# Two attention layers on one core: the second layer's row sums brought to 32 rows per tile by four transfers, one 128x4 product per block, and output products in pairs

## The chip, the cores and the metric

The kernel runs on one core of a Trainium2 chip. The metric is device time in microseconds (us) of one execution; less is better. Before the change the median of three runs is 3128.35 us (3128.15 to 3134.23).

## What is computed

Four images of 4096 tokens with 256 channels pass through two attention layers, all in fp32:

```python
q, k, v = x @ Wq + bq, x @ Wk + bk, x @ Wv + bv            # layer 0; q, k: 32 wide, v: 256
x = gamma * softmax(q @ k.T) @ v + x
g, f, v = x @ Wg + bg, x @ Wf + bf, x @ Wh + bh            # layer 1; g, f: 32 wide, v: 128
x = x + (softmax(g @ f.T) @ v) @ Wo + bo
```

No maximum is taken off before the exponential. The softmax's denominator is divided out at the end, so the kernel needs, for each query, the sum of the exponentials over 4096 keys.

## The kernel before

The program is one long unrolled list of 1024 **steps**: four images `b`, in each layer 0 and then layer 1. Layer 0 has 16 blocks `j` of 256 queries with 8 steps each, layer 1 has 8 blocks of 512 queries with 16 steps `i` each; a step of layer 1 takes 256 keys against 512 queries. In a step the TensorE (PE) makes the scores `st` (L621), the ScalarE (ACT) their exponential `p` (L638), and the PE multiplies by the values (L713 in layer 1, L689 in layer 0). Half of the steps of layer 1, the split ones, work with a coarse `high` from ACT (L631) and two remainders `low` (L659) and `d` (L664) from the VectorE (DVE). A split step gives the PE four short passes at once, and two more with the next step; the others give it four long ones.

**Sums.** The `p` of a block are added over its steps. Some steps are added into `p_sum` by the DVE (L678). Those named in `MOVED_SUMS`, or in `MOVED_IMAGE` and `MOVED_LAST` for the last image, are added into `p_sum_moved` by accumulating DMAs on the queue of GpSimd (POOL, L650, L652; L654 joins two such sums in the last image). After the block, `add_moved` (L778) and `fold` (L782) bring all into `sums`: 128 rows by 512 queries, where the 128 rows are still to be added. `later_sums` is a planner's list of these DVE additions, each with a cost and a latest step; `tensor_clock` and `vector_clock` say when one may go.

**Outputs.** A block's outputs are made in the next block. `output(t)` has three stages for each of four 128-query tiles: `multiply` puts the product of `o` and `wo` (L799, 128x256) and the product of the tile of `sums` with a column of ones (L800, 128x1, which adds the 128 rows) into one PSUM buffer `pso`; `divide` is the reciprocal on the DVE (L803); `give` is the scaled copy to `y` on ACT (L807), and an accumulating DMA from POOL that adds `y` to the rows of `out` (L809). This is done for 31 blocks. The last block of all has code of its own (`last_sums`, `last_denominators`, `last_outputs`: L838 to L872), which is not changed.

**Order.** From step 8 on the order is written by hand: each engine, and each DMA queue (SP's and POOL's), takes its instructions in program order. `put(n, slot, ...)` hangs a stage on step n: slot "a" is at the step's start, slot "b" behind the scores of the step two ahead and ahead of the step's own products. `OUT_AT = (9, 10, 12, 13)` are the steps of the next block in which the four tiles are multiplied; `divide` follows in slot "a" and `give` in slot "b" of the next step. The last block of an image has its outputs in steps 1 to 4 of the next image's layer 0, the block before the last of all in `LAST_OUT_AT`. PSUM buffers of the tag `side` (two) are shared by `pso` and the projections `psv` (L497) and `psqk` (L446); SBUF buffers of the tag `small` (four) by `y`, `x_res` and others. SP's queue carries the loads for the projections (`xT_again` L917, `squares` L290, `x_res` L1007), POOL's the accumulating DMAs and the loads of `q` and `k` (L543).

Of the kernel before, what the change touches and what calls it, by code (L numbers as in the profile page):

```python
# [50 lines left out]
F32 = mybir.dt.float32  # L51
F32R = mybir.dt.float32r
I32 = mybir.dt.int32
AF = mybir.ActivationFunctionType
ALU = mybir.AluOpType
AX = mybir.AxisListType

P = 128
QB = 512
QB0 = 256  # L60
NT = QB // P
S = 32
# [1 line left out]
EPS = 2.0**-12  # L64
UP = 2.0**12
AHEAD = 3
OUT_AT = (9, 10, 12, 13)
LAST_OUT_AT = (5, 6, 7, 8)
MOVED_AT = 1
KEEP, AHEAD_OF = 3, 1.0  # L70
Q_AHEAD = 6
# [179 lines left out]
def fast_path(ctx: ExitStack, tc: tile.TileContext, x, w0, w1, wo, bo, gamma, out, off):  # L251

    nc = tc.nc
    B, N, C = x.shape
# [9 lines left out]
    NS = QB0 // P  # L264
# [7 lines left out]
    const = ctx.enter_context(tc.tile_pool(name="const", bufs=1))  # L272
    data = ctx.enter_context(tc.tile_pool(name="data", bufs=1))
    work = ctx.enter_context(tc.tile_pool(name="work", bufs=2))
    dram = ctx.enter_context(tc.tile_pool(name="dram", bufs=1, space=bass.MemoryType.DRAM))
# [25 lines left out]
    rows = {}  # L301
# [18 lines left out]
    nc.sync.dma_start(ident_dram, ident)  # L320
    ones = const.tile([P, 1], F32, name="ones")
    nc.vector.memset(ones, 1.0)

    inverse = const.tile([P, 2, B * N // P], F32, name="inverse")
    seen_v = const.tile([P, 2, B * NH], F32, name="seen_v")
# [8 lines left out]
    wo_sb = const.tile([P, C], F32, name="wo")  # L334
# [20 lines left out]
    def side_psum(name):  # L355
        return ps_side.tile([P, QB], F32, tag="side", name=name)
# [3 lines left out]
    for j in range(NB):  # L360
        forms = {}
        for what, col in (("h", 1.0), ("l", 0.0), ("d", -EPS)):
            t = const.tile([P, NT, W], F32R, tag=f"v0{what}_{j}", name=f"v0{what}_{j}")
# [24 lines left out]
    q_t, moved_sums, first_p, later_sums, v_whole = {}, {}, [], [], {}  # L388
# [3 lines left out]
    def put(n, slot, *stages):  # L392
        todo.setdefault((n, slot), []).extend(stages)
# [167 lines left out]
    last_block = B * PER_IMAGE - NI[1]  # L561
# [30 lines left out]
    def small(name):  # L592
        return work.tile([P, C], F32, tag="small", bufs=4, name=name)
# [171 lines left out]
    def take_first_two(b, j, acc):  # L765

        o = []
        for h in range(QB // QB0):
            o.append(work.tile([P, W], F32, tag="o", name=f"o_{b}_{j}_{h}"))
            nc.scalar.activation(o[h][:, :QB0], acc[0][:, h * QB0 : (h + 1) * QB0], AF.Copy, scale=1.0 + EPS)  # L770
        return o

    def end_second(b, j, acc, p_sum, o, n_next):
        key = f"{b}_{j}"
        sums = [None]

        def add_moved():
            nc.vector.tensor_add(p_sum, p_sum, moved_sums[b, j, 0])  # L778

        def fold():  # L780
            sums[0] = work.tile([P, QB], F32, tag="sums", bufs=1, name=f"sums_{key}")
            nc.vector.tensor_add(sums[0].rearrange("p (a n) -> p a n", n=QB0), p_sum[:, :NS, :], p_sum[:, NS:, :])  # L782

        wait = j < NQ[1] - 1
        if not wait:
            while later_sums:
                later_sums.pop(0)[2]()
        for h in range(QB // QB0):
            nc.vector.tensor_add(o[h][:, :QB0], o[h][:, :QB0], acc[1][:, h * QB0 : (h + 1) * QB0])  # L789

        def output(t):
            tok = slice(t * P, (t + 1) * P)
            n = (b * N + j * QB) // P + t
            held = {}

            def multiply():
                held["ps"] = ps = side_psum(f"pso_{key}_{t}")
                part = o[t // NS][:, t % NS * P : (t % NS + 1) * P]
                nc.tensor.matmul(ps[:, :C], part, wo_sb, start=True, stop=True)  # L799
                nc.tensor.matmul(ps[:, C : C + 1], sums[0][:, tok], ones[:, :1], start=True, stop=True)  # L800

            def divide():
                nc.vector.reciprocal(inverse[:, 1, n : n + 1], held["ps"][:, C : C + 1])  # L803

            def give():
                y = small(f"y_{key}_{t}")
                nc.scalar.activation(y, held["ps"][:, :C], AF.Copy, scale=inverse[:, 1, n : n + 1])  # L807
                row = j * QB + t * P
                nc.gpsimd.dma_start(out[b, row : row + P, :], y, accum_op=ALU.add)  # L809

            return multiply, divide, give

        out_at = (1, 2, 3, 4) if not wait else OUT_AT if n_next < last_block else LAST_OUT_AT
        if wait:
            put(n_next + MOVED_AT, "b", lambda: later_sums.append((1.15, n_next + MOVED_AT + 3, add_moved, None)))
            put(n_next + MOVED_AT, "b", lambda: later_sums.append((0.6, n_next + MOVED_AT + 4, fold, f"p_sum_{b}_{j}")))
        else:
            put(n_next, "b", add_moved, fold)
        for t in range(NT):
            multiply, divide, give = output(t)  # L820
            at = n_next + out_at[t]
            put(at, "b", multiply)
            put(at + 1, "a", divide)
            put(at + 1, "b", give)

    ending = {}

# [64 lines left out]
    def put_all(n, at, stages):  # L892
        for where, stage in zip(at.split(), stages):
            put(n + int(where[:-1]), where[-1], stage)
# [63 lines left out]
    acc, p_sum, o = None, None, []  # L958
    tensor_clock, vector_clock = 0.0, 0.0
# [27 lines left out]
    for n, s in enumerate(steps):  # L987
        now[0] = n
        b, l, j = s.b, s.l, s.j
# [4 lines left out]
        if s.first:  # L994
            o = []
# [6 lines left out]
        if l == 0 and s.i == NI[0] - 3:  # L1002
            x_res[b, j] = []
            for t in range(NS):
                x_res[b, j].append(small(f"x_res_{b}_{j}_{t}"))
                row = (j * NS + t) * P
# [7 lines left out]
        if ahead is not None and ahead.first:  # L1014
            k = (ahead.b, ahead.l, ahead.j * (QB0, QB)[ahead.l] // QB)
# [13 lines left out]
        if l == 0:  # L1029
            s.cut_both()  # L1030
            after.cut_low()
        else:
            cost = 1.9 if s.split else 2.2
            tensor_clock += cost + 1.7 * (b + 1 < B and s.i in (3, 7)) + 0.63 * (j > 0 and s.i in OUT_AT)
            vector_clock = max(vector_clock, tensor_clock - cost)
            s.cut_both()
            after.cut_low()
            vector_clock += 1.15 * (s.split + after.split)
            if n < len(steps) - 2:
                s.add_up(p_sum)  # L1040
        if l == 1:
# [4 lines left out]
            if s.last:  # L1046
                o = take_first_two(b, j, acc)
# [5 lines left out]
            while later_sums and (later_sums[0][1] <= n or vector_clock + later_sums[0][0] <= tensor_clock + AHEAD_OF):  # L1053
                took, _, issue, _ = later_sums.pop(0)
# [12 lines left out]
            if n == len(steps) - 1:  # L1067
                last_outputs(acc, o)
            elif s.last:
                vector_clock += 0.8  # L1070
                end_second(b, j, acc, p_sum, o, n + 1)
# [23 lines left out]
def tile_two_attention_layers(tc: tile.TileContext, *args):  # L1095
    nc = tc.nc
    with tc.tile_pool(name="flag", bufs=1) as pool:
        off = pool.tile([1, 1], I32, name="off")
        fast_path(tc, *args, off)
        flag = nc.values_load(off[0:1, 0:1], min_val=0, max_val=4 * P, skip_runtime_bounds_check_because="a count")  # L1100
        with tc.If(flag < 1, preferred_fallthrough_block=False, label="in_range") as usual:
            pass
        with usual.Else():
            general_path(tc, *args)
# [40 lines left out]
```

## Time and profile before

| | us |
|---|---|
| median of three runs | 3128.35 |
| the profiled execution, its own time | 3129.13 |
| its span in the trace | 3127.4 |
| a block of layer 1, images 0 to 2 (640.0 to 678.5) | 38.5, of it PE 38.50, DVE 34.27, ACT 27.99, POOL 10.50 |
| a block of layer 1, image 3 (2973.5 to 3008.5) | 35.0, of it PE 35.00, DVE 29.64, ACT 25.64, POOL 12.92 |
| layer 0 of image 1 (836.2 to 1332.3) | 496.1, of it PE 494.50, DVE 444.44, ACT 349.77 |

The granted TensorE clock is 0.999 over the span. Blocks are counted here from the copy of the first accumulator (L770) that ends a block's products. Times in the profile are from the span's start. PE instructions in fp32 with full precision are recorded as two passes (L799 and L800: 124 products, 248 records); DMA groups give the KB of one transfer and the median us from issue to landing.

### The profile page before, as it was taken

The numbers are of one execution on the slowest core, as the hardware profiler recorded it, in microseconds if no ns is written. First come the engines' busy times: TensorE is split into PE (matmuls) and PEld (weight loads), VectorE is DVE, ScalarE is ACT, GpSimd is POOL, SyncE is SP. The second block draws the span as 40 slices with busy tenths as digits, with TensorE's granted clock in tenths as the row PEclk, the third lists the DMA queues.
The fourth block names the chain that finished last, engine by engine and source line by source line (L and its number), as shares of the span: only waits on it lengthen the run. The fifth ranks groups of instructions, "written<-read, shape, count | busy, mean of one in ns | idle before, by whom it ended". The sixth has DMA issues, their size and how long they took to land.

```text
span 3127.4 us, 55023 instructions
## 1 busy us (share of the span) xinstructions
PE 3093.8 (99%) x20052; PEld 2692.9 (86%) x20052; DVE 2732.4 (87%) x3328; ACT 2203.5 (70%) x2900; POOL 791.8 (25%) x1157
## 2 busy tenths in 40 slices
PE   8999999999999999999999999999999999999998
PEld 7999999666799999866679999986668999997665
DVE  6899889988888989998889988998888888888887
ACT  7767777777677777777767777677776666667775
POOL 4111113222411111422241111132234111123332
PEclk9999999999999999999999999999999999999999
DMA  4344455656644444656554444465565333337776
GB/s 124 75 89 89 84 96 115 127 115 118 125 85 84 93 89 87 128 121 118 117 110 92 84 89 90 88 133 115 115 128 97 63 70 72 60 76 158 154 154 140
DMA packets 441606, 325.86 MB, mean 104 GB/s; under 512 B 264466, under 2 KB 386196, under 8 KB 441332
## 3 DMA queue, kind: packets, MB, share of 16 engines
q0 software_dynamic: 112272, 196.49, 34.9%
q1 hardware_dynamic: 328148, 125.47, 16.8%
q8 instruction: 162, 2.65, 0.4%
q14 instruction: 112, 0.92, 0.1%
q10 hardware_dynamic: 912, 0.33, 0.1%
HBM read 128.45 MB, written 95.49 MB: 72 GB/s over the span
## 4 chain that ended last, share of the span: by engine, by line
PE 88%; DVE 3%; DMA 3%; issue 2%; ACT 2%; POOL 1%; SPq 0%; DVEq 0%; POOLq 0%; ACTq 0%
PE acc L689 23%; PE acc_pair L689 23%; PE acc L713 21%; PE st L621 14%; PE psv L497 4%; DMA p_sum_moved<-p 2%; PE psqk L446 2%; PE pso L799 1%; POOL k L543 1%; ACT p L638 0%; PE pso L800 0%; DVE d L664 0%; DVE low L659 0%; DVE p_sum L678 0%; ACT v0l L524 0%
## 5 line engine op out<-in xcount | busy, mean ns | idle before, releaser
L631 ACT ACTIVATE high<-st,down 128x1024 fp32r<-128x1024 f32 x651 | 728.2, 1119 | 686.9 <-PE st L621 609.1
L638 ACT ACTIVATE p<-st 128x1024 f32<-128x1024 f32 x1024 | 1028.9, 1021 | 20.3 <-DMA p_sum_moved<-p 9.3
L659 DVE TENSOR_TENSOR low<-p,high 128x1024 fp32r<-128x1024 f32 x565 | 690.7, 1223 | 144.4 <-ACT p L638 136.8
L664 DVE SCALAR_TENSOR_TENSOR d<-low,high 128x1024 fp32r<-128x1024 f32 x547 | 667.5, 1220 | 15.3 <-PE acc L713 0.7
L621 PE MATMUL st<-q,k 128*128 128x256 f32 (+1 forms) x3072 | 661.5, 323 | 0.6 <-DMA q<-qk_dram 0.5
L621 PEld LDWEIGHTS st<-q,k 128*128 128x128 f32 x3072 | 472.1, 189 | 57.5 <-issue 8.1
L713 PE MATMUL acc<-p,v 128*128 128x512 f32 (+1 forms) x1028 | 487.6, 596 | 0.8 <-DVE o L789 0.7
L689 PE MATMUL acc<-v0d,d 128*128 128x258 f32 x2048 | 336.5, 286 | 5.0 <-DVE d L664 4.7
L689 PE MATMUL acc<-v0h,high 128*128 128x258 f32 x2048 | 330.9, 284 | 1.2 <-ACT high L631 1.2
L689 PE MATMUL acc_pair<-v0l,low 128*128 128x256 f32 (+1 forms) x2048 | 329.9, 283 | 0.0
L689 PE MATMUL acc_pair<-v0h,high 128*128 128x258 f32 x2048 | 329.6, 283 | 0.0
L689 PE MATMUL acc<-v0l,low 128*128 128x256 f32 (+1 forms) x2048 | 328.1, 282 | 1.1 <-DVE low L659 0.8
L689 PE MATMUL acc_pair<-v0d,d 128*128 128x258 f32 x2048 | 328.8, 282 | 0.0
L754 POOL DMA_DIRECT2D out<-x x128 | 114.8, 897 | 839.3 <-DVE x L748 831.4
L713 PEld LDWEIGHTS acc<-p,v 128*128 128x128 f32 x1028 | 187.6, 189 | 143.1 <-issue 124.4
L678 DVE TENSOR_TENSOR p_sum<-p_sum,p 128x1024 f32<-128x1024 f32 x239 | 291.2, 1219 | 0.5
L689 PEld LDWEIGHTS acc<-v0d,d 128*128 128x128 f32 x2048 | 280.9, 189 | 7.8 <-DVE d L664 5.9
L689 PEld LDWEIGHTS acc<-v0h,high 128*128 128x128 f32 x2048 | 281.5, 189 | 3.0 <-ACT high L631 1.4
L689 PEld LDWEIGHTS acc<-v0l,low 128*128 128x128 f32 x2048 | 280.9, 189 | 2.6 <-DVE low L659 2.6
L689 PEld LDWEIGHTS acc_pair<-v0l,low 128*128 128x128 f32 x2048 | 282.4, 189 | 0.1
L689 PEld LDWEIGHTS acc_pair<-v0h,high 128*128 128x128 f32 x2048 | 281.9, 189 | 0.2 <-DVE o L733 0.2
L689 PEld LDWEIGHTS acc_pair<-v0d,d 128*128 128x128 f32 x2048 | 281.6, 189 | 0.0
(173 smaller groups left out, 4231.6 us busy)
## 6 DMA issues: line engine op xcount, KB each, us to landing
p_sum_moved<-p POOLq DMA_DIRECT2D x207, 512.0 KB, 5.0
x_res<-in_x SPq DMA_DIRECT2D x128, 128.0 KB, 3.2
qk_dram<-qk_parts SPq DMA_DIRECT2D x128, 128.0 KB, 2.2
x_res<-bias POOLq DMA_DIRECT2D x128, 128.0 KB, 4.1
out<-bias SPq DMA_DIRECT2D x128, 128.0 KB, 4.0
out<-x POOLq DMA_DIRECT2D x128, 128.0 KB, 3.1
q<-qk_dram POOLq DMA_DIRECT2D x252, 64.0 KB, 4.0
out<-y POOLq DMA_DIRECT2D x124, 128.0 KB, 3.5
```

The lines of the kernel that those rows point to most:

```text
L446: nc.tensor.matmul(t["ps"], wqk[l][:, c, :], x_parts[key][n][:, c, :], start=(c == n == 0), stop=(c == NCC - 1 and n == 1),)
L497: nc.tensor.matmul(ps[:, n, :], xT[key][:, c, n * P : (n + 1) * P], wv[l][:, c, :], start=(c == 0), stop=(c == NCC - 1),)
L543: nc.gpsimd.dma_start(dst[n * D : (n + 1) * D, :], parts[h, which])
L621: nc.tensor.matmul(st[:, g, :], k_t[b, l, kt // NT][:, kt % NT * P : (kt % NT + 1) * P], q_t[b, l, j * n // QB][:, q0 : q0 + n], start=Tru ...
L631: nc.scalar.activation(self.high, s_flat, AF.Exp, bias=down)
L638: nc.scalar.activation(self.p, s_flat, AF.Exp)
L659: nc.vector.tensor_sub(self.low, self.p, self.high.bitcast(F32))
L664: nc.vector.scalar_tensor_tensor(self.d, self.low.bitcast(F32), -UP, self.high.bitcast(F32), ALU.mult, ALU.add)
L678: nc.vector.tensor_add(p_sum, other, self.p)
L689: nc.tensor.matmul(acc[2 * s + which][:, :width], p[:, g, s * P : (s + 1) * P], v0[self.i][v][:, g, :width], start=self.first and what != ...
L713: nc.tensor.matmul(acc[which].rearrange("p (a n) -> p a n", n=QB0)[:, cols, :], v_part[:, g, :], p[:, g * NS : (g + 1) * NS, :][:, cols, : ...
L754: nc.gpsimd.dma_start(out_rows(b, j, s), x_new, accum_op=ALU.add)
```

## The change

The 128 rows of `sums` are no longer added by the PE alone. `fold_rows` adds rows 64 to 127 onto rows 0 to 63 by an accumulating DMA on POOL's queue; `store_rows` writes the 64 rows to DRAM from SP's queue; `gather(0)` reads 32 of them back from SP's queue, so that tile t of the queries lies on partitions 32t to 32t+31 of a 128x128 buffer `rows`; `gather(1)` adds the other 32 by an accumulating DMA on POOL's queue. Each waits for the one before. Then one product of `rows` with a constant 128x4 matrix (`quarters`) gives the block's four columns of sums (`count`), and one reciprocal of 128x4 takes the place of four of 128x1. The output products of two tiles share one `pso` buffer. The stages have new steps: transfers in slots 5a, 5b, 6b, 7b, `count` in 11b, the pairs in 12b and 14b, each given one step later; behind an image's last block 1a, 1b, 2b, 3a, then 5b, 5b and 6b. The planner's two deadlines come one step earlier, and its cost for the outputs is 0.86 in two steps for 0.63 in four.

```diff
-OUT_AT = (9, 10, 12, 13)
-LAST_OUT_AT = (5, 6, 7, 8)
+OUT_AT = (11, 12, 14)
+FIRST_OUT_AT = (5, 5, 6)
+GATHER_AT = "5a 5b 6b 7b"
+FIRST_GATHER_AT = "1a 1b 2b 3a"
...
+    quarters = const.tile([P, NT], F32, name="quarters")
+    nc.vector.memset(quarters, 0.0)
+    for t in range(NT):
+        nc.vector.memset(quarters[t * S : (t + 1) * S, t : t + 1], 1.0)
...
+        def fold_rows():
+            nc.gpsimd.dma_start(sums[0][: P // 2, :], sums[0][P // 2 :, :], accum_op=ALU.add)
+
+        def store_rows():
+            held["dram"] = dram.tile([P // 2, QB], F32, name=f"sums_dram_{key}")
+            nc.sync.dma_start(held["dram"], sums[0][: P // 2, :])
+
+        def gather(k):
+            def issue():
+                if k == 0:
+                    held["rows"] = small(f"rows_{key}")[:, :P]
+                part = held["dram"][k * S : (k + 1) * S, :].rearrange("r (t q) -> t r q", q=P)
+                if k == 0:
+                    nc.sync.dma_start(held["rows"], part)
+                else:
+                    nc.gpsimd.dma_start(held["rows"], part, accum_op=ALU.add)
...
+        def count():
+            held["ps"] = ps = side_psum(f"ps_sums_{key}")
+            nc.tensor.matmul(ps[:, :NT], held["rows"], quarters, start=True, stop=True)
+
+        def divide():
+            nc.vector.reciprocal(inverse[:, 1, n : n + NT], held["ps"][:, :NT])
+
+        def output(h):
             def multiply():
-                held["ps"] = ps = side_psum(f"pso_{key}_{t}")
-                part = o[t // NS][:, t % NS * P : (t % NS + 1) * P]
-                nc.tensor.matmul(ps[:, :C], part, wo_sb, start=True, stop=True)
-                nc.tensor.matmul(ps[:, C : C + 1], sums[0][:, tok], ones[:, :1], start=True, stop=True)
+                held[h] = ps = side_psum(f"pso_{key}_{h}").rearrange("p (s c) -> p s c", c=C)
+                for s in range(NS):
+                    nc.tensor.matmul(ps[:, s, :], o[h][:, s * P : (s + 1) * P], wo_sb, start=True, stop=True)
             def give():
+                for s in range(NS):
...
-            put(n_next + MOVED_AT, "b", lambda: later_sums.append((1.15, n_next + MOVED_AT + 3, add_moved, None)))
-            put(n_next + MOVED_AT, "b", lambda: later_sums.append((0.6, n_next + MOVED_AT + 4, fold, f"p_sum_{b}_{j}")))
+            put(n_next + MOVED_AT, "b", lambda: later_sums.append((1.15, n_next + 3, add_moved, None)))
+            put(n_next + MOVED_AT, "b", lambda: later_sums.append((0.6, n_next + 4, fold, f"p_sum_{b}_{j}")))
...
+        put_all(n_next, gather_at, (fold_rows, store_rows, gather(0), gather(1)))
+        put(n_next + out_at[0], "b", count)
+        put(n_next + out_at[0] + 1, "a", divide)
+        for h, at in enumerate(out_at[1:]):
+            multiply, give = output(h)
+            put(n_next + at, "b", multiply)
+            put(n_next + at + 1, "b", give)
...
-            tensor_clock += cost + 1.7 * (b + 1 < B and s.i in (3, 7)) + 0.63 * (j > 0 and s.i in OUT_AT)
+            tensor_clock += cost + 1.7 * (b + 1 < B and s.i in (3, 7)) + 0.86 * (j > 0 and s.i in OUT_AT[1:])
```

More of the change, by code (lines that the diff above doesn't have):

```diff
@@ L789, in end_second @@
             nc.vector.tensor_add(o[h][:, :QB0], o[h][:, :QB0], acc[1][:, h * QB0 : (h + 1) * QB0])
[L791 to L794, printed above, removed]
-            def multiply():
-                held["ps"] = ps = side_psum(f"pso_{key}_{t}")
-                part = o[t // NS][:, t % NS * P : (t % NS + 1) * P]
[L799 to L803, printed above, removed]
-            def give():
[L806 to L811, printed above, removed]
@@ L813, in end_second @@
-        out_at = (1, 2, 3, 4) if not wait else OUT_AT if n_next < last_block else LAST_OUT_AT
+        held = {}
+        def fold_rows():
[12 more added lines that the diff above has]
+                    nc.gpsimd.dma_start(held["rows"], part, accum_op=ALU.add)
+            return issue
@@ new lines, in end_second @@
+        n = (b * N + j * QB) // P
+        def count():
[4 more added lines that the diff above has]
+        def output(h):
+            def multiply():
+                held[h] = ps = side_psum(f"pso_{key}_{h}").rearrange("p (s c) -> p s c", c=C)
+                for s in range(NS):
+                    nc.tensor.matmul(ps[:, s, :], o[h][:, s * P : (s + 1) * P], wo_sb, start=True, stop=True)
+            def give():
+                for s in range(NS):
+                    t = h * NS + s
+                    y = small(f"y_{key}_{t}")
+                    nc.scalar.activation(y, held[h][:, s, :], AF.Copy, scale=inverse[:, 1, n + t : n + t + 1])
+                    row = j * QB + t * P
+                    nc.gpsimd.dma_start(out[b, row : row + P, :], y, accum_op=ALU.add)
+            return multiply, give
@@ L814, in end_second @@
+        out_at, gather_at = (OUT_AT, GATHER_AT) if wait else (FIRST_OUT_AT, FIRST_GATHER_AT)
         if wait:
-            put(n_next + MOVED_AT, "b", lambda: later_sums.append((1.15, n_next + MOVED_AT + 3, add_moved, None)))
-            put(n_next + MOVED_AT, "b", lambda: later_sums.append((0.6, n_next + MOVED_AT + 4, fold, f"p_sum_{b}_{j}")))
+            put(n_next + MOVED_AT, "b", lambda: later_sums.append((1.15, n_next + 3, add_moved, None)))
+            put(n_next + MOVED_AT, "b", lambda: later_sums.append((0.6, n_next + 4, fold, f"p_sum_{b}_{j}")))
@@ L817, in end_second @@
         else:
             put(n_next, "b", add_moved, fold)
[L819 to L824, printed above, removed]
+        put_all(n_next, gather_at, (fold_rows, store_rows, gather(0), gather(1)))
[5 more added lines that the diff above has]
+            put(n_next + at + 1, "b", give)
```

## The prediction

> **What bounds the kernel now.** I read the shares of busy time first, then the busy time by stretches, then the chain of waits inside one block, then the DMA groups and the last block.
>
> ```profile
> PE 3093.8 (99%) x20052; PEld 2692.9 (86%) x20052; DVE 2732.4 (87%) x3328; ACT 2203.5 (70%) x2900; POOL 791.8 (25%) x1157
> ```
>
> A share over the whole span could hide a stage with another limit, so next come the stretches of one block of layer 1 in images 0 to 2, and of one in image 3 (columns: length, then busy PE, PEld, DVE, ACT, POOL, clock, DMA share, GB/s):
>
> ```profile
> 640.00:678.50 38.50, 38.50 (x145) 26.52 (x144) 34.27 (x38) 27.99 (x38) 10.50 (x14) 1.00 0.57 112
> ...
> 2973.50:3008.50 35.00, 35.00 (x129) 23.44 (x128) 29.64 (x32) 25.64 (x32) 12.92 (x17) 1.00 0.79 158
> ```
>
> The PE is never idle in either; the DVE has 4.2 us to spare in the first and 5.4 us in the second. Anything that leaves the PE here shortens the block, until something else is late. The chain inside such a block (start, us, what) tells what an output tile costs:
>
> ```profile
> 657.07 1.73 PE psv L497 x8
> ...
> 665.65 0.47 PE st L621 x2
> 666.12 0.43 PE pso L799 x2
> 666.55 0.12 PE pso L800 x2
> 666.67 1.05 PE acc L713 x4
> 667.71 0.46 PE st L621 x2
> ...
> 675.71 0.46 PE st L621 x2
> 676.17 0.93 PE acc L713 x4
> 677.10 0.47 PE st L621 x2
> ```
>
> From scores to scores a split step with an output takes 667.71 - 665.65 = 2.06 us, one without 677.10 - 675.71 = 1.39 us: an output tile costs 0.66 us (the long steps say the same: 3.30 against 2.65). The eight 256-column passes of `psv` take 1.73 us, 0.216 each, so the two passes of L799 are 0.43 us. What is left, **0.23 us, is the product with the ones**: 0.12 at its own place and 0.11 by which the product behind it comes later.
>
> **The change on the PE.** Per block three of four such products go; the fourth, now 128x4, I keep at 0.23 us (four columns, the same weight load). The wo products stay, four by 0.43; in pairs they stand as `psv`'s passes do, for 0.216 a pass. So 2.64 us become 1.95, a gain of 0.69 us; with the measured 0.224 (2.047 - 1.391 - 0.432, medians over all such steps) it is 0.67. For 30 blocks 20.2 us; the 31st is taken apart below. The nearest other price for a one-column product is the busy time of its group, 34.4 us for 124, 0.28 us each, which would make 25 us; its own 0.12 us alone would make 11 us. I take 20.2.
>
> The Trainium skill speaks against so much: "TensorE: Matmul & The Clock Gate", section "Back-to-back issue gap", gives a product of 1 to 64 columns some 25 ns, so 0.05 us in two passes; by that the whole gain would be 4.7 us, and the time about 3124. The rows above have 0.23 us, and decide.
>
> Three stalls of the PE go besides: in the last block of images 0 to 2 the outputs of steps 9 and 10 wait for a `side` buffer that `psv` of step 9 holds ("PE pso L799 <- DVE v0d L533: 2.7, 3"). The new steps are clear of it. But ACT there waits for `p_sum_moved` (1.4 us before 820.6), and that lateness may show at the next product, so I count 1.7 of 2.7 us.
>
> **DVE and ACT.** The DVE's order is unchanged but for three reciprocals fewer (0.48 us a block): the planner had issued `add_moved` and `fold` before both deadlines. So `sums` is ready when it was: the DVE ends L782 at 650.22 in the block of 640.0, at 2984.47 in that of 2973.5. In step 15 ACT now has two copies (2 x 0.48) where one was; the `low` of step 2 ends 1.0 us before the PE takes it, so this is hidden, barely. The five new memsets lie in the start, beside loads; nothing.
>
> **The four transfers.** They are new waits, on queues where others stand behind. What the PE sees is one thing: `count` in slot 11b is in order, and if `rows` has not landed, everything behind it waits, scores included. The time allowed from the end of L782 to `count` (its old place less the 0.66 us of each output that no longer precedes it):
>
> - images 0 to 2, inside layer 1: 666.9 - 650.2 = 16.6 us
> - into layer 0 of the next image: 857.5 - 843.4 = 14.1 us
> - image 3, shorter steps: 2996.6 - 2984.5 = **12.2 us**
>
> Where the allowance of image 3 begins (the DVE's timeline), and the groups of DMAs nearest to the four (KB of one, us to landing):
>
> ```profile
> 2983.78 0.69 DVE L782 TENSOR_TENSOR sums<-p_sum 128x512 f32<-128x512 f32 x1
> ```
> ```profile
> qk_dram<-qk_parts SPq DMA_DIRECT2D x128, 128.0 KB, 2.2
> x_res<-bias POOLq DMA_DIRECT2D x128, 128.0 KB, 4.1
> ...
> out<-x POOLq DMA_DIRECT2D x128, 128.0 KB, 3.1
> q<-qk_dram POOLq DMA_DIRECT2D x252, 64.0 KB, 4.0
> ```
>
> None of the four is in the trace, so each is bounded by rows (least to most, us). `fold_rows`: 1.7 (`k<-qk_parts`, 32 KB, not accumulating) to 5.6 (`x_res<-bias`, accumulating); I take 3.5, between the medians of the accumulating rows. `store_rows`: 1.7 to 4.9 (`qk_dram<-qk_parts`); 2.2. `gather(0)`: 1.6 (`squares`, 32 KB) to 4.0; 2.1. `gather(1)`: 1.9 (`q<-qk_dram`) to 7.5; 3.6. POOL goes on 0.5 us behind a landing (653.14 to 653.68), SP 0.1. Sum: 0.15 + 3.5 + 0.1 + 2.2 + 0.1 + 2.1 + 0.5 + 3.6 = **12.3 us**, ends 7.2 and 22.8. So it is hidden with 4 us to spare in images 0 to 2, with 2 at their ends, and stands just at its limit in image 3. There I count 0.5 us in each of six blocks, 3 us.
>
> The Trainium skill has a shorter chain: "DMA: Bandwidth & Descriptors", section on the anatomy of one DMA, fits 2.0 us plus bytes over 436 GB/s; the four would take 8.9 us and `count` would never wait, 3 us better than my sum. The accumulating rows above, at 3.1 to 4.1 us for 128 KB, do not agree.
>
> Queued behind: on POOL, `fold_rows` waits for L782 ahead of the move of p of step 5, and `gather(1)` waits for `gather(0)` ahead of that of step 9 (image 3: step 8). In images 0 to 2 the moves wait longer for one another's landing (4.5 to 5.1 us each), so nothing is added. In image 3 the move of step 8 goes from 2989.7 to about 2995, but that of step 11, which waits for its landing, goes at 2999.4 anyway. In an image's last block POOL also loads `k` between the moves (26 us busy of 40.7), and on SP `xT_again` of step 9 stands behind `gather(0)`: it lands about when `psv` wants it; 1 us for the three.
>
> **The last block** has another limit; the chain there is of transfers:
>
> ```profile
> 3099.99 6.13 DMA p_sum_moved<-p
> ...
> 3106.64 4.90 DMA p_sum_moved<-p_sum_moved
> ...
> 3111.64 1.24 DVE p_sum L838
> ```
>
> PE time saved there is worth nothing. `fold_rows` and `gather(1)` come into this very chain, and `gather(1)` ahead of the move of step 8 puts it off by about 0.9 us: a loss of 0.9.
>
> **Sum.** 3129.1 - 20.2 - 1.7 + 3 + 1 + 0.9 = 3112.1 by the profiled execution, which was 0.8 above the median of the runs: **3111 us**.
>
> **Rivals.**
>
> - *`rows` late in image 3 alone* (0.14). The allowance is 12.2 us, and the DMA engines there are 0.79 busy against 0.57 to 0.62; a landing of `out<-y`, 3.5 us in the median, takes 5.0 there (2974.3 to 2979.4). Each link 0.75 us slower makes 3 us more in each of six blocks: 3129.
> - *`rows` late everywhere, slower than before* (0.06). The place is the same, `count` in 11b; it decides from a chain of 15 us on, where seven blocks of image 3 lose 2.8 us each and three ends of layers 0.9, the whole gain. With each link at its ninth decile (4.8, 3.9, 3.0, 4.8, waits 0.9) it takes 17.4 us: 0.8 us late in 21 blocks, 3.3 in three ends of layers, 5.2 in seven blocks of image 3, 63 us, which with the gain makes about 3170. For it speaks that four transfers in a row each see the moves of 512 KB in flight; against it that `xT_again`, 256 KB, lands in 2.9 us (649.0 to 651.9) with such a move in flight.
> - *The product costs its own 0.12 us only* (0.08), the rest being paid by any product that ends such a row of passes: 3111 + 9 = 3120. Against it stands `psv`, which ends so too, at 0.216 a pass.
> - *Another engine takes over* (0.04): the DVE at 34.3 of 38.5 us would have to wait on something in turn, as its 0.4 us before the `d` of step 0 allows. No change, 3128.
>
> That the change does not do what it says can be left out: in its instruction order the products, the reciprocals and the transfers stand where the text puts them.
>
> **Numbers.** The forecast has 0.68, its own range 3104 (all 2.7 us of the stalls, no lateness in image 3) to 3119. To hold 8 in 10 it reaches on into the first rival: 3104 to 3124. This kernel's measurement can tell 0.2%, 6.3 us, from no change: faster means under 3122.1, slower over 3134.6. Faster: the forecast, the third rival and 0.05 of the first, 0.81; same: 0.07 of the first and the fourth, 0.11; slower: the second and the last 0.02 of the first, 0.08.
>
> **What would show it.** In the profile after: blocks of images 0 to 2 at 37.8 us, of image 3 at 34.3 to 35.0; a step with a pair longer by 0.86, that with `count` by 0.23; PE idle before `count`, ended by the landing of `rows`, zero in images 0 to 2 and under 1 us each in image 3; no wait of L799's successor for `v0d`. I am wrong if blocks of images 0 to 2 keep 38.5 us, if `count` waits there, or if ACT's waits for `p_sum_moved` (9.3 us in all now) grow by several us.

## The result

| | before | after |
|---|---|---|
| median of the runs, us | 3128.68 (6 runs, 3127.75 to 3134.23) | 3196.68 (6 runs, 3195.26 to 3201.74) |
| profiled execution, us | 3129.13 | 3195.26 |
| span, us | 3127.4 | 3193.5 |
| granted clock | 0.999 | 0.988 |

After over before is 1.0215 (95% interval 1.0202 to 1.0229). The forecast of 3111 us was wrong, in sign too.

The profile after begins with the same shares, busy time of each engine and its part of the span. The PE is busy for 7.8 us more, with fewer instructions, in a span that is 66 us longer. So it is idle for 58 us more than before, and its instructions take longer somewhere:

```profile
PE 3101.6 (97%) x19866; PEld 2686.9 (84%) x19866; DVE 2729.7 (85%) x3240; ACT 2204.8 (69%) x2900; POOL 856.2 (27%) x1219
```

The stretches say where. First the block of images 0 to 2 that was shown before, then the last block of image 0, then a block of image 3, the one ahead of that shown before and as long there, 35.0 us (columns as before: length, busy PE, PEld, DVE, ACT, POOL, clock, DMA share, GB/s):

```profile
640.90:678.70 37.80, 37.80 (x140) 25.97 (x139) 34.21 (x34) 28.11 (x38) 12.78 (x17) 1.00 0.68 129
...
796.80:842.40 45.60, 41.54 (x154) 28.89 (x153) 35.77 (x36) 29.80 (x41) 27.17 (x48) 0.96 0.73 142
...
2968.90:3009.80 40.90, 36.68 (x123) 23.82 (x123) 29.57 (x28) 25.65 (x32) 15.63 (x21) 0.92 0.73 145
```

The ordinary block went from 38.5 to 37.8 us, as the prediction said. The last block of image 0 went from 40.7 to 45.6, and that of image 3 from 35.0 to 40.9. In both the PE is idle for 4 us, and the clock has fallen: in image 3 the PE is busy for 36.68 us where it was for 35.0 before. The PE's waits over the whole span (total us, times, longest) name the two places:

```profile
PE ps_sums L822 <- DMA rows<-sums_dram: 37.6, 10, 6.3
PE psv L503 <- DMA xT_again<-xT_dram: 20.7, 6, 6.3
```

36.3 us of the first line are the seven blocks of image 3 (3.8 to 6.3 each); the rest is three waits of 0.3 to 0.6 in images 0 to 2. The second line is the last two blocks of images 0 to 2.

**The chain in a block of image 3**, from the timelines of POOL and of SP's queue (start, us, what; the idle time before it in brackets):

```profile
2981.30 0.85 POOL L800 DMA_DIRECT2D sums<-sums  x1 [5.64 <-DVE sums L788]
2981.87 2.16 POOL L658 DMA_DIRECT2D p_sum_moved<-p  x2
2993.47 1.12 POOL L814 DMA_DIRECT2D rows<-sums_dram  x1 [9.44 <-DMA rows<-sums_dram]
2994.16 2.25 POOL L658 DMA_DIRECT2D p_sum_moved<-p  x2
2995.27 3.19 POOL L549 DMA_DIRECT2D q<-qk_dram  x4
```
```profile
2984.05 0.47 SPq L804 DMA_DIRECT2D sums_dram<-sums  x1
2989.96 0.56 SPq L812 DMA_DIRECT2D rows<-sums_dram  x1
```

`fold_rows` had held up two moves of p (the DMAs of 512 KB that add `p` to `p_sum_moved`); they follow it at 2981.87. `store_rows` goes out behind them at 2984.05, and the transfer that waits for it, `gather(0)`, goes out at 2989.96: 5.9 us, where the prediction had 2.2 and 0.1. Then POOL stands still for 9.4 us at `gather(1)`, and two more moves and the four loads of the next block's `q` stand behind it. At 2997.52 the PE takes `count`, after 4.2 us.

Every link, worked out from the issue times and landings (us; 15 chains in blocks 1 to 5 of images 0 to 2, and the seven of image 3):

| link | priced | images 0 to 2 | image 3 |
|---|---|---|---|
| end of the fold to `fold_rows` landed | 0.15 + 3.5 | 3.0 to 3.3 | 3.0 to 3.8 |
| `store_rows`, to the issue of `gather(0)` | 0.1 + 2.2 + 0.1 | 4.1 to 5.1; 2.4 to 3.2 in three blocks | 5.9 to 7.0 |
| `gather(0)`, to the issue of `gather(1)` | 2.1 + 0.5 | 3.2 to 4.9 | 3.5 (5.0 in one) |
| `gather(1)` to its landing | 3.6 | 4.3 to 6.8 | 4.0 to 4.6 |
| all | 12.3 | 15.5 to 17.1 | 16.5 to 18.6 |
| allowed | 16.6 and 12.2 | 16.4 to 16.6 | 12.1 to 12.2 in six of seven (experiment 4, which does not wait) |

So images 0 to 2 just get by, and image 3 does not. Where the store's time goes, the DMA queues show. In block 6 of image 0 the store is issued at 770.22, behind a move issued at 769.45. From 770.3 to 773.4 the DMA engines move packets of POOL's queue alone (`q0`; packets, MB, share of 16 engines), and none of SP's:

```profile
q0 software_dynamic: 128, 0.52, 90.6%
```

**The last two blocks of images 0 to 2.** SP's queue in block 6 of image 0, and the PE's first instruction that waits:

```profile
770.22 0.47 SPq L804 DMA_DIRECT2D sums_dram<-sums  x1
774.67 0.56 SPq L812 DMA_DIRECT2D rows<-sums_dram  x1
775.32 0.90 SPq L948 DMA_DIRECT2D xT_again<-xT_dram  x2
```
```profile
781.07 1.13 PE L503 MATMUL psv<-wv,xT_again 128*128 128x256 f32 x4 [2.68 <-DMA xT_again<-xT_dram]
```

The load of `xT_again` was due at 7b, but SP waits at `gather(0)` for the store to land, 4.45 us, and goes on to the load only then. Here the clock stays up; at a wait of 3.1 us in image 1 (1553.8 to 1556.8) it does not:

```profile
776.62:780.03 3.41, 1.76 (x8) 1.00 0.98 196
780.03:783.45 3.42, 2.38 (x10) 1.00 0.70 158
...
1554.87:1558.28 3.41, 1.44 (x7) 1.00 0.62 152
1558.28:1561.69 3.41, 3.41 (x8) 0.50 0.97 170
```

These are stretches of 3.41 us (length, busy PE, clock, DMA share, GB/s); why of this length comes below.

**The clock.** The stretches of 2 us around the wait of 4.2 us in image 3:

```profile
2993.00:2995.00 2.00, 0.30 (x2) 1.00 0.00 0
2995.00:2997.00 2.00, 0.00 (x0) 0.57 0.67 93
2997.00:2999.00 2.00, 1.48 (x4) 0.50 1.06 196
2999.00:3001.00 2.00, 2.00 (x5) 0.50 1.07 188
3001.00:3003.00 2.00, 2.00 (x7) 0.72 1.04 195
3003.00:3005.00 2.00, 2.00 (x11) 1.00 1.16 219
```

The clock halves while the PE waits, and stays halved for 4.6 us after it. The first row shows one thing more: no byte moves there. POOL goes on to `gather(1)` at 2993.47 only, and its bytes move from 2995 on. The chain has both kinds of time: while the store stands behind the two moves the DMA engines are full, and later they are all but idle:

```profile
2984.00:2989.00 5.00, 5.00 (x20) 1.00 1.06 199
2990.00:2995.00 5.00, 3.30 (x13) 1.00 0.05 13
```

### The profile page after: what moved, and what is told of

Same layout as the page of the kernel before. It is cut to its first block, busy times and chain, and to the rows that moved or that the text cites. A ratio compares the mean times of both kernels' runs of the same rounds, so it can differ in the third digit from the quotient of the medians.

```text
span 3193.5 us, 54944 instructions
## 1 busy us (share of the span) xinstructions
PE 3101.6 (97%) x19866; PEld 2686.9 (84%) x19866; DVE 2729.7 (85%) x3240; ACT 2204.8 (69%) x2900; POOL 856.2 (27%) x1219
## 3 DMA queue, kind: packets, MB, share of 16 engines
q1 hardware_dynamic: 334720, 131.57, 17.1%
## 4 chain that ended last, share of the span: by engine, by line
PE 83%; DMA 7%; DVE 3%; issue 3%; ACT 2%; POOL 1%; SPq 0%; DVEq 0%; POOLq 0%; ACTq 0%
PE acc L695 22%; PE acc_pair L695 22%; PE acc L719 19%; PE st L627 13%; PE psv L503 4%; DMA rows<-sums_dram 3%; PE psqk L452 2%; PE pso L831 2%; DMA sums_dram<-sums 1%; ACT p L644 1%; POOL k L549 1%; DMA p_sum_moved<-p 1%; DMA xT_again<-xT_dram 1%; DVE p_sum L684 0%; DVE d L670 0%
## 5 line engine op out<-in xcount | busy, mean ns | idle before, releaser
L719 PE MATMUL acc<-p,v 128*128 128x512 f32 (+1 forms) x1028 | 498.9, 609 | 0.4 <-DVE o L795 0.2
L719 PEld LDWEIGHTS acc<-p,v 128*128 128x128 f32 x1028 | 196.0, 194 | 147.2 <-issue 128.4
```

Source lines behind the costliest of these rows:

```text
L719: nc.tensor.matmul(acc[which].rearrange("p (a n) -> p a n", n=QB0)[:, cols, :], v_part[:, g, :], p[:, g * NS : (g + 1) * NS, :][:, cols, : ...
```

## The experiments

Theory: the saving on the PE is real, and the loss is waits for transfers that stand in queues. Rivals: the traffic of the four transfers itself, the pairs of outputs, or a saving that was never there. "After" is the changed kernel; times are medians, ratios are to the kernel before, with 95% intervals.

**1. Image 3 by the old way** (`a1_image3_old`); `output_one` is the `output` of the kernel before, at its steps; the planner has its old cost there.

```diff
+        old = b == B - 1
+        if old:
...
+            for t in range(NT):
+                multiply, divide, give = output_one(t)
...
+            return
         put_all(n_next, gather_at, (fold_rows, store_rows, gather(0), gather(1)))
```

> The new way stays for the blocks of images 0 to 2; the seven blocks of image 3 make their denominators as before (four products with the ones column, no transfers). My theory, that the PE's waits for the landing of rows in image 3 and the halved clock behind each of them cost 47.4 us (291.4 us for the seven blocks against 244.0): those blocks go back to 35.0 us, and the time is 3195.3 - 47.4 = about 3148 us. Rival, that the four transfers slow the kernel by their traffic wherever they run: image 3 improves, but the blocks of images 0 to 2 show the loss too; the rest of it, 24 us, would then be spread over all of them. Rival, that the loss of image 3 sits in the shared output buffers and not in the transfers: the same 3148, so a kernel that keeps the pairs and does not wait for rows is run beside it.

Measured 3151.06 us, 1.0069 (1.0044 to 1.0093). The seven blocks are back at 35.5, 35.8, 35.0, 35.4, 35.1, 35.1 and 32.5; images 0 to 2 are as in after, the ordinary blocks (1 to 5) at 37.2 to 39.2 us (37.2 to 38.6 in after, 38.4 to 39.1 in the kernel before). The traffic rival falls there, in images 0 to 2.

**2. The load of `xT_again` ahead of the transfers** (`a2_fetch_early`).

```diff
-        put(m - 2, "b", fetch)
+        put(m - (5 if m % NI[1] == 9 else 2), "b", fetch)
```

> The third load of xT_again of the last two blocks of images 0 to 2 is issued three steps earlier, so that it stands ahead of the two transfers on SP's queue. My theory, that psv waits there because the load stands behind the second of them, which waits for the first to land: the PE's waits for xT_again (20.8 us in six blocks) go, the last two blocks of those images fall from 42.4 to 48.8 us to some 39.4 to 41, and the time is 3195.3 - 24 to 28 = 3167 to 3171 us. Rival, that the load is late by the traffic of the transfers and not by its place on the queue: the load takes as long as before from issue to landing, the PE still waits, and the time stays over 3185.

Measured 3178.99 us, 1.0163 (1.0142 to 1.0183): between the two. The waits for `xT_again` are gone, all 20.7 us, and the blocks before the last take 39.4 us. But in the last blocks (44.1, 47.0 and 44.7 us) `count` now waits in its turn, 2.2, 3.8 and 1.8 us. One wait was hiding another.

**3. Both** (`a3_both`; the two diffs above).

> Both edits: image 3 by the old way, the third load of xT_again ahead of the transfers. My theory adds the two: 3195.3 - 47.4 - 26 = about 3122 us, under the kernel before by 0.67 us for each of some 18 to 24 blocks less 3 us by which the first layer starts later. Rival, that the saving of 0.67 us a block is given back elsewhere: 3129 us or more.

Measured 3130.08 us, 1.0003 (0.9994 to 1.0013). 8 us short of the theory. In part it is what was just seen: the last blocks (44.1, 45.6 and 44.5 us, before 40.6, 41.0 and 42.2) give back what the others saved; and layer 0 of image 2 with the block behind it takes 501.0 us, before 497.2. The time is the rival's.

**4. The transfers issued, and not waited for by `count`** (`a4_unused`).

```diff
-            nc.tensor.matmul(ps[:, :NT], held["rows"], quarters, start=True, stop=True)
+            nc.tensor.matmul(ps[:, :NT], sums[0][:, :P], quarters, start=True, stop=True)
```

> The four transfers are all issued, but the 128x4 product reads the first tile of the folded sums in place of what they bring, so nothing on the PE waits for the last three of them; the denominators are not those of the reference. My theory, that it is the wait and not the traffic that costs: no block of image 3 waits, they take 34.3 to 35 us, and only the waits for xT_again stay: 3195.3 - 50 = about 3145 us. Rival, that the transfers' traffic and the pairs of outputs cost the time: over 3180 us.

Measured 3192.17 us, 1.0200 (1.0182 to 1.0218). My theory fell here, by 47 us. Six of the seven blocks of image 3 take as long as in after (40.4 to 43.7 us). The seventh has no load of `q` to wait for and takes 33.0, but the PE then waits 6.2 us for the last block's sums. The PE's waits in the six are now:

```profile
PE st L627 <- DMA q<-qk_dram: 32.3, 6, 6.6
```

The loads of `q` for the next block stand on POOL's queue behind `gather(1)` (seen in the timeline above) and come late by as much as `rows` does. So `count` was only the first to pay. The new theory: what costs is that `gather(1)`, issued at 7b, holds POOL's whole queue until `gather(0)` has landed; the rival is still the traffic. Experiments 7 to 9 bear on it.

**5. No transfers at all** (`a5_no_transfers`): the edit of 4, and

```diff
-        put_all(n_next, gather_at, (fold_rows, store_rows, gather(0), gather(1)))
```

> The four transfers are not issued at all; the 128x4 product reads the first tile of the folded sums, so the denominators are not the reference's. It is the change's saving on the PE by itself. Theory of the prediction (0.67 us a block, 20 us, and 1.7 us of stalls): 3128.2 - 22 = 3106 us, up to 3110 with the start of layer 0 behind the pairs of steps 5 and 6. Rival, that an output product behind another one costs less than thought or that the saving is given back: 3120 us or more. With the kernel in which the transfers are issued and not waited for by the product (3192 us) it tells what the transfers alone cost.

Measured 3114.84 us, 0.9957 (0.9941 to 0.9972); its profiled execution has a span of 3109.1, 18.3 under that of before. The PE's saving by itself, a block of images 0 to 2 and one of image 3:

```profile
637.00:674.70 37.70, 37.70 (x140) 25.86 (x139) 34.22 (x34) 28.00 (x37) 9.67 (x13) 1.00 0.59 116
2924.50:2958.70 34.20, 34.20 (x124) 22.85 (x123) 29.55 (x28) 25.66 (x31) 13.57 (x18) 1.00 0.82 163
```

0.8 us a block. By steps (medians from scores to scores) a pair makes a step longer by 0.86 us and `count` one by 0.22, where the prediction had 0.86 and 0.23: the price of the ones-products held. The pairs stand in this kernel too, so their rival falls with it. Most of what is missing against 3106 lies where a layer ends: layer 0 with the first block of layer 1 takes 497.2, 501.4 and 489.8 us, before 496.2, 497.2 and 488.2, and within the 501.4 the PE waits 3.6 us for `low` 7 us behind the layer's start.

**6. The new way only where it had room** (`a6_new_in_18`): as 2, and `old = b == B - 1 or j > 5`.

> The new way only where the transfers had room: blocks 0 to 5 of images 0 to 2 (their outputs are made in blocks 1 to 6), the old way for blocks 6 and 7 and for image 3; the third load of xT_again goes ahead of the transfers on SP's queue. Theory, that 18 blocks keep 0.7 us each and nothing else is touched: 3128.2 - 12.6 = 3115.6 us, 3114 to 3119. Rival, that the layer's last block and the start of the next layer lose time whatever way they make their outputs: 3125 us or more.

Measured 3120.22 us, 0.9970 (0.9960 to 0.9980). This beats both kernels: 8 us under before, of the 12.6 expected. Of the rest 2.9 us are five waits of `count` for `rows`, in the blocks that just get by.

**7. Image 3 by the new way, the last transfer later** (`a7_late_in_image3`): as 6, but `old = j > 5`, and

```diff
-        out_at, gather_at = (OUT_AT, GATHER_AT) if wait else (FIRST_OUT_AT, FIRST_GATHER_AT)
+        out_at, gather_at = ((14, 14, 15), "5a 5b 6b 11a") if b == B - 1 else (OUT_AT, GATHER_AT) if wait else (FIRST_OUT_AT, FIRST_GATHER_AT)
```

> As the kernel with the new way in 18 blocks, and in image 3 the new way too, in six blocks, with the last of the four transfers at 11a in place of 7b, the 128x4 product at 14b and the pairs at 14b and 15b. Theory, now that the PE was seen to wait for q of the next block where the product did not wait for rows: in image 3 everything behind the last transfer on POOL's queue is late, because it stands there some 10 us until the one before it has landed; issued at 11a, behind the load of q, it holds up nothing, rows has 4 us to land, and the six blocks take 34.3 to 35.2 us: 3115.6 - 2 to 4 = 3112 to 3114 us. Rival, that the traffic beside 1 MB of moved p is what makes everything late: those blocks keep over 38 us, and the time is over 3130.

Measured 3122.41 us, 0.9979 (0.9970 to 0.9988). The same four transfers beside the same traffic, and blocks of 32.6, 35.7, 34.9, 35.0, 34.8 and 37.4 us where after had 40.8 to 43.4. The traffic rival falls. Nothing is gained over 6: the pair at 15b waits 0.4 us for the reciprocal, since `count` and the pairs share two buffers, and one load of `q` still comes 2.2 us late.

**8. As 7, the last transfer back at 7b** (`a11_gather_at_7b`; one word, `11a` to `7b`).

> As the kernel that makes the 128x4 product at 14b in image 3 and issues the last transfer at 11a (3122.4 us), but with the last transfer back at 7b. Theory, that POOL's queue is the second place where image 3 loses: the transfer at 7b waits there some 10 us, the load of q behind it is late, the PE waits 4.5 to 6.6 us in each of the six blocks for q although it no longer waits for rows, and the time is about 3122 + 6 x 6 = 3155 to 3165 us. Rival, that the later product alone had cured image 3: 3122 us.

Measured 3169.17 us, 1.0121 (1.0106 to 1.0137). `count` at 14b never waits, and the six blocks take 39.8 to 44.1 us all the same:

```profile
PE st L628 <- DMA q<-qk_dram: 35.7, 6, 6.9
```

The slot of one DMA is worth 47 us; nothing else differs from 7. That is POOL's queue, shown.

**9. Without the moves issued right behind `fold_rows`** (`a8_moves_left_out`).

```diff
-                else:
+                elif i != 5 and not (self.late and i == 6):
                     nc.gpsimd.dma_start(moved_sums[b, j, order % both], self.p, accum_op=ALU.add)
```

> The changed kernel without the moves of p that are issued right behind the first transfer: step 5 in images 0 to 2, steps 5 and 6 in image 3 (their sums are missing from the denominators). Theory, that the second transfer takes 4.4 us there and 5.9 to 7.0 in image 3 because the moves of 512 KB are in flight ahead of it: it takes 2.4 us everywhere, the chain falls by 2 us in images 0 to 2 and by 3.5 to 4.6 in image 3, the waits for rows there from 3.8 to 6.3 us to 0.3 to 2, short of halving the clock, and the time to about 3195 - 38 = 3157 us. Rival, that the store is slow by itself (64 rows to DRAM): the chain stays, and the time is over 3185.

Measured 3128.18 us, 1.0001 (0.9992 to 1.0010). SP's queue in the block of image 3:

```profile
2976.46 0.47 SPq L804 DMA_DIRECT2D sums_dram<-sums  x1
2978.83 0.56 SPq L812 DMA_DIRECT2D rows<-sums_dram  x1
```

`store_rows` takes 2.4 us in place of 5.9, and 2.3 to 2.7 in 30 of 31. The chain in image 3 is 13.0 to 13.6 us in five blocks of seven, and the PE waits 12.7 us there in place of 36.3. In images 0 to 2 the chain did not fall by the 2 us expected: it stays at 15.6 to 16.5 us in 14 of the 15. There `gather(0)` now has the next move of p ahead of it (at 1342.61 by 0.94 us, for one) and takes 5.9 to 6.4 us in place of 3.2 to 4.9. I had expected 3157, 29 us more than measured; the waits for `xT_again` fell as well, from 20.7 to 1.8 us, since that load stood behind the same store. This run also takes away POOL work and traffic, so its whole time is not the price of the store alone; its link times are what it shows.

**10. `count` at 13b in image 3** (`a9_count_13`): as 7, `(13, 14, 15)`, the early load in block 6 alone (by 11 this is worth nothing).

> As the kernel that issues the last transfer at 11a in image 3, with the 128x4 product at 13b in place of 14b, so that the pair at 14b has a free buffer, and the early load of xT_again in block 6 alone. Theory, that in image 3 the saving was eaten by the pair's wait for the reciprocal (0.4 us a block): its blocks take 34.3 to 34.6 us in place of 34.9, which makes 2 to 4 us, and the whole 3116 to 3120 us. Rival, that rows has not landed by 13b: the blocks take 36 us or more, and the time is over 3125.

Measured 3136.51 us, 1.0027 (1.0017 to 1.0036). A miss: `rows` lands behind 13b, the PE waits 1.7 to 3.9 us in each of the six blocks, and they take 35.3 to 40.1 us. None of the slots tried in image 3 (11b, 13b, 14b) suits both the landing and the buffers.

**11. As 6, the early load in block 6 alone** (`a10_fetch_early_in_6`).

```diff
-        put(m - (5 if m % NI[1] == 9 else 2), "b", fetch)
+        put(m - (5 if early else 2), "b", fetch)
...
-                        put_values(n + m, b + 1, first + k)
+                        put_values(n + m, b + 1, first + k, j == 6 and m == 9)
```

> As the kernel with the new way in 18 blocks, with the load of xT_again moved ahead of the transfers in block 6 alone; in block 7, where no transfer is, it stays in its old place. Theory, that the three last blocks (43.2, 43.1 and 41.9 us against 40.7, 41.0 and 42.2 before) lose 2 us each by that load: 3120.2 - 5 = 3115 us. Rival, that it is the boundary of the blocks that moved, and the load is innocent: 3120 us within 2.

Measured 3120.40 us, 0.9973 (0.9961 to 0.9984). The rival was right: the last blocks stay at 42.6, 43.2 and 41.9 us. What moved, at least in part, is the boundary, the copy on ACT: the stretch of the last block of image 0 holds 38 passes of scores and 86 of values, before 36 and 82. From the end of the first block to the end of the last this kernel takes 2536.9 us and before 2548.7, 11.8 less, which is 18 times 0.66; the medians differ by 8.7.

## Why the prediction was wrong

**What held.** The bound (the PE, never idle in the ordinary blocks), the 0.67 us of a block (0.7 to 0.8 in most blocks of after and of 5, and 0.68 by the steps of 5), the allowance of image 3 (12.2; measured 12.1 to 12.2), and that no stall for `v0d` is left at an output product in the last blocks. So the saving is there: 18.3 us by the spans of experiment 5. Against this price the prediction set the 25 ns of the Trainium skill, "TensorE: Matmul & The Clock Gate", section "Back-to-back issue gap". By the same section that is the gap of a product alone, and for small products it counts too little, having no weight load in it. So the page did not speak against the rows. Two sums of the prediction are off, and nothing rests on them: the lower end of the chain adds up to 7.7 us, not 7.2, and the two items named for 3104 give about 3107.

**What failed, by size.** Experiment 5 has the same PE program without the transfers, so after less 5 is what they cost: 3193.5 - 3109.1 = 84.4 us, where the prediction had 3 + 1 + 0.9. (What the last block of all lost is within the first row. The blocks 1 to 5 of images 0 to 2 cost 3.2 us, the layers 0 took 3.4 us less, and the end 0.3 more.)

| where | after | 5 | cost | of it waits of the PE | the rest |
|---|---|---|---|---|---|
| seven blocks of image 3 | 291.5 | 237.7 | 53.8 | 36.3 | 17.5 |
| last two blocks of images 0 to 2 | 268.3 | 241.1 | 27.2 | 20.7 | 6.5 |
| up to the first block's end | 565.37 | 562.03 | 3.3 | | |

The last row differs as much from execution to execution (561.5 to 564.3 in the other kernels; in this one the clock halved at 94 us, behind waits of the start) and is not put down to the change.

**First failed step: "`store_rows`: 1.7 to 4.9; 2.2".** It takes 4.1 to 5.1 us in most blocks of images 0 to 2, at the upper end of that range, and 5.9 to 7.0 in image 3, beyond it. The bounds came from groups over the whole program, most of whose members meet no move of p. In after, a store with no move in flight takes 2.3 to 2.7 us; behind one issued 0.5 us or more ahead of it, it lands after that move, mostly by 0.5 us; in image 3, where `fold_rows` had dammed up two, 0.3 to 0.8 before the second. The prediction set this aside with a row of its own: `xT_again`, 256 KB, "lands in 2.9 us (649.0 to 651.9) with such a move in flight". That row was misread. The move was issued at 649.06, just *behind* the load. The trace of before also has the other case, at 770.08, with the move issued 0.88 us *ahead* (DMA issues of that stretch, then of the first; KB, us to landing):

```profile
p_sum_moved<-p POOLq DMA_DIRECT2D x1, 512.0 KB, 5.3
xT_again<-xT_dram SPq DMA_DIRECT2D x1, 256.0 KB, 4.9
```
```profile
p_sum_moved<-p POOLq DMA_DIRECT2D x1, 512.0 KB, 4.1
xT_again<-xT_dram SPq DMA_DIRECT2D x1, 256.0 KB, 2.9
```

With 5.9 for 2.2 the chain of image 3 would have come to 16.0 us, over the 15 from which the text itself said the change would lose. The two gathers were priced too low as well, by 1.3 to 1.9 us together in six of the seven chains of image 3; `fold_rows` was not.

**Second failed step: "Queued behind".** On POOL the moves were looked at, and the four loads of `q` behind them were not; by 4 and 8 those cost as much as `rows`. On SP the text had `xT_again` land "about when `psv` wants it; 1 us for the three"; it is 20.7 us, in six blocks, because `gather(0)` waits there for a store that stands behind a move.

**Third, missed altogether: a long wait costs more than itself.** 24 us of the 84 (17.5 + 6.5) are work at half the clock: in those blocks the PE was busy for 48 us at 0.50. In layer 1 of after the waits of 2.7 us and less left the clock at 1.00, and behind each of the eleven of 3.1 us and more it stood at 0.50 for 3.41 us (three times) or 6.83 us (eight times).

The length of the wait does not decide by itself: in experiment 4 one of 2.6 us was followed by 3.41 us at 0.50, and at the start of after three waits of 0.5, 1.6 and 1.2 us within 5 us by 6.83. What fits is a grid. In each of the thirteen traces all falls of the clock lie on one grid of 3.41 us, which stands at another place in each run. In after, of the windows of this grid at 1.00, each in which the PE was idle for 1.97 us or more is followed by one at 0.50, and none of those idle for 1.78 us or less. Over all traces, with 57 falls ahead of the programs' ends, the two cases meet between 1.1 and 2.0 us. The wait of 2.7 us was cut in two by the grid, 1.65 and 1.04 us, as the rows above show; that of 3.1 us had 1.97 in one window.

The Trainium skill, "TensorE: Matmul & The Clock Gate", Part 1, has this rule: after about 3.4 us of idleness the array runs at half rate, until it has been busy for as long. The traces agree on the 3.4 us as the length of a window, and not on the idleness: at the wait of 4.2 us the clock fell 2.0 us after the wait had begun.

**The rivals.** "Rows late everywhere", given 0.06, comes nearest. It had "5.2 in seven blocks of image 3", 36.4 us, and the PE waited 36.3; its chain of 17.4 us is the middle of the 16.5 to 18.6 measured. That the sum fits so well is luck: it put every link at its ninth decile, `fold_rows` at 4.8 us (measured 2.7 to 2.9) and `store_rows` at 3.9 (5.9 to 7.0). In images 0 to 2 it was wrong: there `rows` is in time, and SP's queue and the clock cost the rest. "Late in image 3 alone" had the place, with a third of the price (18 us of 53.8).

**Open.** That of the 84 us so much is due to each of the two queues is not settled: their waits hide one another, as 2 and 4 show, so the single prices do not add. Nor was the wait at the start of layer 0 (experiment 5) taken apart, nor is it shown why the store stands behind the move's bytes in place of taking turns with them.

## What to carry to other kernels

Price a transfer by a row of the trace that has the same traffic *ahead* of it at its issue, and look at who was issued first, not at who overlaps. For every DMA that waits, list all that stands behind it on its queue up to the next landing that somebody needs, and give each a due time; a place in the order was worth 47 us here (7 against 8). Where a matmul-bound kernel may be made to wait 2 us or more, count for the clock too: 24 us came on top of 57 us of waits here.

## What the runs showed of the hardware

- A transfer on SP's queue landed behind a large one of POOL's that was issued 0.5 us or more before it: 128 KB took 2.3 to 2.7 us alone and 4.4 to 4.5 behind 512 KB issued 0.8 us earlier. Behind two such (image 3) it landed after the first and 0.3 to 0.8 us before the second. The Trainium skill, "DMA: Bandwidth & Descriptors", section "Queues, rings and completion order", says that each DMA engine takes packets of its queues in turn, by which the small transfer would be expected to land well before the large one. It landed 0.5 us after it, and in the 3.1 us behind its issue none of its packets moved; the measurement decides.
- An accumulating transfer within SBUF (128 KB) landed in 2.7 to 2.9 us in 30 of 31 cases, one from DRAM into SBUF of half the bytes (64 KB, pieces of 512 bytes) in 4.0 to 6.8. The fit that the Trainium skill gives in "DMA: Bandwidth & Descriptors", section "Anatomy of one DMA — SWDGE (gpsimd) path", is for transfers issued from GpSimd. By it these two would take an estimated 2.3 and 2.2 us, which is near for the first alone; of the two on SP's queue, which the prediction priced by it too, it says nothing.
- A PE wait of 4.2 us made its block 6.7 us longer than the same block without transfers (40.9 against 34.2).
- All falls of the clock in a run lie on one grid of 3.41 us, and but for the one at the program's end the stretches at 0.50 last one to three of its windows. In after the clock fell 2.0 to 5.2 us after a wait of 3.1 us or more had begun; a window with 1.97 us of idleness was enough.
